# A list scheduler in the kernel's source: weights from traces and eight transfer lanes in place of a table of offsets

## The chip, the cores and the metric

The kernel runs on one core of one Trainium2 chip. The metric is the device time of one execution in microseconds, as the median of several runs. Engines are named as in the profile: PE (TensorE, matmuls), PEld (its weight loads), DVE (VectorE), ACT (ScalarE), POOL (GpSimd) and SP (SyncE, which here issues most transfers). Each engine works off its own instructions in the order in which the program has them.

## What is computed

Two layers on x of shape (4, 256, 64, 64), all in float32. Layer 0 is a Mamba block over 4 x 4096 tokens of 256 channels with an inner width of 512 and 16 states per channel. Layer 1 is a second state-space block, with 8 heads of 64, followed by a mixture of 8 experts in which each token goes to one expert of limited capacity.

```python
# layer 0, per token l (cut)
tokens = x.transpose(0, 2, 3, 1).reshape(B, L, C) @ w_in.T
z = sigmoid(silu(tokens @ w_gate.T + b_gate))
t = layernorm(tokens); xm, zm = split(t @ in_w.T)
xm = silu(causal_conv4(xm)); dt = softplus(...); Bss, Css = ...
h = exp(dt * A) * h + (dt * xm) * Bss          # 512 x 16 states
y = (h * Css).sum(-1) + D * xm
out = tokens + (y * silu(zm) @ out_w.T) * z @ w_out.T + x
# layer 1 (cut)
zxbcdt = rmsnorm(ln(t)) @ W_in.T               # then conv4, silu, softplus
state = state * dA + dt * x B ;  y = state C + D x
t = t + ln(t) + rmsnorm(y * silu(z)) @ W_out.T
# experts (cut)
e = argmax(softmax(ln(t) @ gate_w + gate_b))
t = t + prob * (relu(ln(t) @ w1[e] + b1[e]) @ w2[e] + b2[e])   # up to a capacity per expert
```

## The kernel before

The kernel has three phases. `mixers` does both state-space layers and the routing, `experts` works through blocks of 256 routed tokens, and `turn` transposes the result back into channels-first layout. Only `mixers` is touched here.

`mixers` cuts the 16384 tokens into 64 chunks of 256. A chunk runs through stages, each a Python function: `front0` (input products, first convolution), `mid0` (softplus, and the step sizes, inputs and B and C are written to DRAM in another layout), `scan` (the recurrence of layer 0), `tail0`, `front1` (second layer's products and convolution), `ssd` (its chunked recurrence) and `back1` (output, routing, a scatter of rows to the experts' buffer). Chunk i's layer 0 is recorded together with chunk i-2's `ssd` and `back1`.

A chunk's `scan` has 16 units, four channel groups j by four state groups f. A unit is:

- on ACT, four exponentials into `da` (the decay; three buffers);
- on DVE, the product `ub` = u x B into PSUM (one buffer), a small add into its first column (`ub<-ub,e`, the carry from the chunk before) and the scan itself, `h` (`tensor_tensor_scan`, 1024 columns);
- on ACT, a copy of the last column, `hlast`;
- on POOL, the product `p` = h x C (two buffers), and on PE the sum over states into `py`, which DVE multiplies into `g` once for every two channel groups.

Nothing of this is issued when it is written down. The class `Plan` records every operation as an `Op` with an engine, a weight (its planned duration), the operations that it depends on and a slot (its priority). `Plan.order` then runs a list scheduler: each engine takes, among the operations whose inputs are ready in the plan and whose buffers are free, the one with the lowest slot. `Plan.issue` emits the program in the order of the planned starts. The plan's times decide the order alone; on the chip an instruction starts when its engine gets to it and its semaphores allow.

What the change touches in it:

- The weights, by a formula in each recording method: `mm`, `transpose`, `act`, `copy`, `dve`, `gps`, `scatter`.
- `SIGNAL`, the time from the end of an operation to when another engine can use it; a later operation of the same engine could start at once.
- Two rules for the shared memory port of DVE and POOL: an operation with `port` set does not start while the other engine has one under way, and `p`, recorded with `ride=True`, is placed with the start of a scan (which does not use the port) unless it has waited for `PATIENCE`. `issue` then makes `p` wait for the DVE instruction ahead of that scan.
- `SHIFT`, a table of 140 offsets: `Chunk.at(n)` sets the slot of a chunk's n-th stage step to `n` plus the offset under the step's running number.

Of the kernel before, what the change touches and what calls it, by code (L numbers as in the profile page):

```python
# [20 lines left out]
P = 128  # L21
# [22 lines left out]
TAIL, SSD, BACK = 18, 29, 37  # L44
AHEAD = 4

SHIFT = {
    1: -2.3, 4: 1.4, 5: 0.2, 6: -1.3, 7: -0.3, 8: -0.3, 9: -0.3, 10: -0.3, 11: -0.3, 12: -0.3, 14: -0.3, 15: -0.3,
    16: -0.3, 17: -0.3, 18: -0.3, 19: -0.3, 20: -0.3, 21: -0.3, 22: -0.3, 23: -0.3, 24: -0.3, 25: -0.3, 26: -3.3,
    27: -2.2, 28: 0.2, 29: -0.1, 30: -2.2, 31: -2.2, 32: -2.2, 33: -2.2, 34: -2.2, 35: -2.2, 36: -2.2, 37: 1.2,  # L50
    38: 0.5, 39: -2.2, 40: -2.1, 41: -2.2, 42: -2.7, 43: -2.2, 44: -2.2, 45: -6.0, 46: -2.2, 47: -2.2, 48: -2.2,
    49: -2.2, 50: -2.2, 51: -2.2, 52: -9.4, 53: -2.2, 54: -1.4, 55: -2.2, 56: -2.2, 57: -2.2, 58: -2.2, 59: -2.2,
    60: -4.7, 61: -2.2, 62: -2.2, 63: -2.2, 64: -2.2, 65: -2.2, 66: -2.2, 67: -2.7, 68: -2.2, 69: -2.2, 70: -2.2,
    71: -0.1, 72: -2.2, 73: -2.2, 74: -2.2, 75: -5.9, 76: -4.8, 77: -2.2, 78: -2.2, 79: -2.7, 80: -2.2, 81: -2.2,
    82: -2.2, 83: -2.2, 84: -2.2, 85: -5.2, 86: -2.2, 87: -2.2, 88: -2.2, 89: -2.2, 90: -2.2, 91: -1.4, 92: -2.2,
    93: -2.2, 94: -2.2, 95: -2.7, 96: -2.2, 97: -2.2, 98: -2.2, 99: -2.2, 100: -2.2, 101: -2.2, 102: -2.2,
    103: -2.2, 104: -2.2, 105: -2.2, 106: -2.3, 107: -4.0, 108: -2.0, 109: -2.2, 110: -2.2, 111: -2.2, 112: -2.2,
    113: -1.8, 114: -1.3, 115: 0.9, 116: -0.3, 117: 1.8, 118: -0.3, 119: 0.1, 120: -0.3, 121: -0.3, 123: -0.3,
    124: -0.3, 125: -0.3, 126: 0.6, 127: -1.2, 128: -0.3, 129: -0.3, 130: 0.3, 131: 0.4, 132: -1.4, 133: -0.3,
    134: -0.3, 135: -0.3, 136: 1.6, 137: -0.3, 140: 0.6,  # L60
}
TOK = 4
ROW = TOK + C

# [85 lines left out]
class Plan:  # L150
# [3 lines left out]

    SIGNAL = 0.15
    SPARE = {}
    PATIENCE = 4.0

# [57 lines left out]

    def mm(self, out, left, right, **kw):
        rows, n = out.shape[0], self.width(right)  # L220
        w = max(0.24, n / 550) if rows > 64 else max(0.16, n / 900) if rows > 32 else max(0.15, n / 1500)
        self.note("PE", w, self.nc.tensor.matmul, (out, left, right), kw, (out,), (left, right), join=out.root)

    def transpose(self, out, src, ident):
        w = 0.08 + 0.1 * src.shape[0] / P
        self.note("PE", w, self.nc.tensor.transpose, (out, src, ident), {}, (out,), (src,), join=out.root)

    def act(self, out, src, func, **kw):
        w = 0.2 + self.width(out) / 1200
        self.note("ACT", w, self.nc.scalar.activation, (out, src, func), kw, (out,), (src, *kw.values()))  # L230

    def copy(self, out, src):
        self.note("ACT", 0.2 + self.width(out) / 1200, self.nc.scalar.copy, (out, src), {}, (out,), (src,))

    def acts(self, weight, calls):

# [4 lines left out]
    def dve(self, name, *args, **kw):  # L241
        out, *rest = (*args, *kw.values())
        tensors = [a for a in rest if isinstance(a, Part) or hasattr(a, "ap")]
        n = max(self.width(a) for a in (out, *tensors))
        port = len([a for a in tensors if self.on_sbuf(a) and self.width(a) > 1]) > 1
        if name == "tensor_tensor_scan":
            n, port = 2 * n, False
        op = self.note("DVE", 0.14 + n / 960, getattr(self.nc.vector, name), args, kw, (out,), rest, port=port)
        op.scan = name == "tensor_tensor_scan"
        if op.scan:  # L250
            self.scans.append(op)
# [2 lines left out]
        self.dve("tensor_tensor", out, a, b, op)  # L254

    def gps(self, name, *args, ride=False, **kw):
        w = 0.3 + self.width(args[0]) * 2.02e-3
        f = getattr(self.nc.gpsimd, name)
        self.note("POOL", w, f, args, kw, (args[0],), args[1:], port=True, ride=ride)

# [6 lines left out]
    def scatter(self, out, rows, src, bound):  # L267


        def f(out, rows, src):  # L270
            return self.nc.gpsimd.indirect_dma_start(
                out=out,
                out_offset=bass.IndirectOffsetOnAxis(ap=rows, axis=0),
                in_=src,
                in_offset=None,
                bounds_check=bound,
                oob_is_err=False,
            )

        self.note("POOL", 1.8, f, (out, rows, src), {}, (out,), (rows, src), lag=4.0)  # L280

    def order(self):
# [8 lines left out]
        free = dict.fromkeys(engines, 0.0)  # L293
        port = {"DVE": 0.0, "POOL": 0.0}

        rings, queues, events = {}, {}, [0.0]
# [4 lines left out]
        for op in self.ops:  # L301
            if not op.missing:
                heappush(waiting[op.engine], (0.0, op.seq, op))
        done = 0
        scan = before = last = shared = None

        def room(op, now):
            for root in op.roots:
                if not root.begun:
                    ring, queue = rings.setdefault(root.ring, []), queues[root.ring]  # L310
                    ring[:] = [o for o in ring if o.left or o.until + self.SIGNAL > now]
                    while queue[-1].begun:
                        queue.pop()
                    if len(ring) + (queue[-1] is not root) * self.SPARE.get(root.ring, root.depth) >= root.depth:
                        return False
            return True

        while done < len(self.ops):
# [6 lines left out]
            for e in engines:  # L325
                while waiting[e] and waiting[e][0][0] <= now:
                    _, _, op = heappop(waiting[e])
                    insort(could[e], (op.slot, op.seq, op))
                if free[e] > now:
                    continue  # L330
                for i, (_, _, op) in enumerate(could[e]):

                    if op.ride and not (scan and now - scan.start < 0.2) and now - op.ready < self.PATIENCE:
                        continue
                    if op.port and port["DVE" if e == "POOL" else "POOL"] > now:
                        continue
                    if room(op, now):
                        break
                else:
                    continue  # L340
                del could[e][i]
                for root in op.roots:
                    if not root.begun:
                        root.begun = True
                        rings[root.ring].append(root)
                op.start, op.end = now, now + op.weight + op.lag
                free[e] = now + op.weight
                heappush(events, free[e])
                if op.port:
                    port[e] = free[e]  # L350
                if e == "DVE":
                    scan = op if op.scan else None
                    before, last = last, op
                    if op.port:
                        shared = op
                elif op.ride:
                    op.behind = before if scan and now - scan.start < 0.2 else shared
                for root in op.roots:
                    root.left -= 1
                    root.until = max(root.until, op.end)  # L360
                    if not root.left:
                        heappush(events, root.until + self.SIGNAL)
                for u in op.users:
                    u.missing -= 1
                    late = op.end if u.engine == e and not op.lag else op.end + self.SIGNAL
                    u.ready = max(u.ready, late)
                    if u.ride and not u.missing:
                        heappush(events, u.ready + self.PATIENCE)
                    if not u.missing:
                        heappush(waiting[u.engine], (u.ready, u.seq, u))  # L370
                        heappush(events, u.ready)
                done += 1
# [16 lines left out]
def tile_conv_attn_hybrid(ctx: ExitStack, tc: tile.TileContext, a: dict, out: bass.AP, cap: int, st: int):  # L389
# [41 lines left out]
    def mixers(es):  # L431
# [220 lines left out]
        def silus(*tiles, gates=0):  # L652

            calls = [(nc.scalar.activation, (t, t, AF.Silu), t, t) for t in tiles]

            calls += [(half_tanh, (t[:, :KC],), t[:, :KC], t[:, :KC]) for t in tiles[:gates]]
            calls.append((nc.scalar.preload_act_table_set, (SETS,), None, None))
            r.acts(sum(0.2 + Plan.width(t) / 1200 for t in tiles) / len(calls) + 2.6 / len(calls), calls)

        def inv_sqrt(dst, src, eps, scale=1.0):  # L660

# [871 lines left out]
```

## Time and profile before

| what | us |
|---|---|
| median of 3 runs (lowest, highest) | 6952.74 (6948.43, 6954.37) |
| the profiled execution | 6966.12 |
| its span, first to last instruction | 6964.3 |
| start of the span to the first scan | 109.4 |
| first scan to last scan (64 chunks x 16) | 5615.8 |
| last scan to the last expert's scatter | 1147.8 |
| turning the result | 91.3 |

The page gives each engine's busy time over the whole span; since the phases differ, the stretch of the scans has to be read by itself. A row of waits says how long an engine sat idle ahead of an instruction and what ended the wait. Idle time shorter than 0.15 us is not put into these rows, so a gap that is short but comes thousands of times shows only in the list of instructions in order of time, where each row has its start and its duration. Durations on DVE reach to the end of the write, and the next instruction may start before that.

### The profile page before, as it was taken

To read this page: it belongs to the slowest core of one execution; us is meant where nothing else is said; L and a number is where in the kernel's file an instruction comes from. 1 tells how busy PE (TensorE), PEld (TensorE's weight loads), DVE (VectorE), ACT (ScalarE), POOL (GpSimd) and SP (SyncE) were. 2 spreads that over 40 slices of the span, in tenths; PEclk is the share of its full clock that TensorE was granted. 3 is DMA by queue.
4 is the path that set the end of the run, shared out by engine and by line. 5 is a ranking of instruction groups with operands and counts; after the bars stand their busy time and mean duration, and the time that the engine had idled before them with its cause. 6 is when DMAs were issued, how large, how long until landed. Compare 5 with 4: busy or idle time off the path is not lost. (4 is left out here: it accounts for less than half of the span.)

```text
span 6964.3 us, 114017 instructions
## 1 busy us (share of the span) xinstructions
PE 6084.7 (87%) x37672; PEld 4128.5 (59%) x37672; DVE 5670.3 (81%) x7646; ACT 4892.5 (70%) x12007; POOL 3431.0 (49%) x2632
## 2 busy tenths in 40 slices
PE   5788888888888888888888888888888877999996
PEld 3455555555555555555555555555555546888886
DVE  4899999999999999999999999999999983434443
ACT  4778888888887778788887777878777863333332
POOL 3455555555555555555555555555555552333331
PEclk7899999999888988998898888989888888999998
DMA  6966667666666666666666666666666633555556
GB/s 178 255 172 178 181 178 182 178 178 178 178 177 173 174 172 176 174 176 171 174 178 177 175 178 176 179 177 176 171 175 176 174 106 132 189 194 197 193 191 238
DMA packets 1125137, 1245.56 MB, mean 179 GB/s; under 512 B 111888, under 2 KB 1093652, under 8 KB 1115330
## 3 DMA queue, kind: packets, MB, share of 16 engines
q1 hardware_dynamic: 1083458, 1008.76, 54.9%
q0 software_dynamic: 30000, 210.98, 8.5%
q10 hardware_dynamic: 11088, 18.53, 0.7%
q8 instruction: 299, 4.90, 0.3%
q14 instruction: 292, 2.39, 0.1%
HBM read 919.92 MB, written 311.63 MB: 177 GB/s over the span
## 5 line engine op out<-in xcount | busy, mean ns | idle before, releaser
L378 POOL TENSOR_TENSOR p<-h,bc 128x1024 f32<-128x1024 f32 x1024 | 2420.7, 2364 | 1980.3 <-DVE ub L378 1371.8
L378 DVE TENSOR_TENSOR_SCAN h<-da,ub 128x1024 f32<-128x1024 f32 x1024 | 2341.8, 2287 | 190.5 <-ACT da L378 69.1
L378 ACT ACTIVATE da<-dt,w_m_Alog 128x255 f32<-128x255 f32 x4096 | 1791.1, 500 | 26.1 <-DVE h L378 17.6
L378 DVE TENSOR_TENSOR ub<-u,bc 128x1024 f32<-128x1024 f32 x1024 | 1370.2, 1338 | 23.9 <-DMA dt<-dt_d 11.5
L378 PE MATMUL py<-p,sum 128*32 128x256 f32 x8192 | 719.0, 434 | 255.2 <-POOL p L378 242.9
L378 PE MATMUL b<-t,w_W_in 128*128 128x256 f32 x2304 | 640.2, 424 | 17.6 <-DVE res L378 10.5
L378 ACT COPY hlast<-h 128x4 f32<-128x4 f32 x1024 | 198.7, 194 | 598.7 <-DVE h L378 596.8
L378 PEld LDWEIGHTS py<-p,sum 128*32 128x32 f32 x8192 | 182.0, 114 | 693.9 <-POOL p L378 399.4
L378 PEld LDWEIGHTS b<-t,w_W_in 128*128 128x128 f32 x2304 | 458.7, 208 | 163.8 <-issue 44.2
L378 PE MATMUL a<-t,w_m_in_w 128*128 128x256 f32 x2048 | 549.8, 422 | 3.5 <-DVE t L378 3.5
L1381 PE MATMUL ph<-xt,w 128*128 128x256 f32 x2272 | 517.1, 381 | 11.5 <-DMA w<-in_w_exp_dram,w_at 6.4
L378 PEld LDWEIGHTS a<-t,w_m_in_w 128*128 128x128 f32 x2048 | 415.9, 211 | 149.5 <-issue 61.0
L1392 PE MATMUL po<-w,hid 128*128 128x256 f32 x2272 | 502.0, 379 | 0.0
L1381 PEld LDWEIGHTS ph<-xt,w 128*128 128x128 f32 x2272 | 427.3, 191 | 70.4 <-ACT hid L1383 7.3
L1392 PEld LDWEIGHTS po<-w,hid 128*128 128x128 f32 x2272 | 431.7, 190 | 58.7
L378 PE MATMUL a<-raw,taps_m 128*32 128x256 f32 x2048 | 211.3, 492 | 234.1 <-DMA raw<-raw_d 169.9
L378 PE MATMUL c<-cum,after 128*128 128x512 f32 x512 | 325.7, 724 | 96.8 <-DVE ex L378 89.9
L1358 DVE CAST number<-rows 128x2 uint32<-128x2 f32 x71 | 12.0, 170 | 476.1 <-DMA tok_d<-fixed,number 461.4
L1356 ACT ACTIVATE tn<-rows 128x256 f32<-128x256 f32 x142 | 82.5, 597 | 414.0 <-DMA rows<-buf_d,row_at 413.5
L1404 POOL DMA_INDIRECT tok_d<-fixed,number x142 | 145.9, 1028 | 390.0 <-DVE fixed L1402 307.6
L378 ACT ACTIVATE cum<-upto,da 128x128 f32<-128x128 f32 x1024 | 337.4, 396 | 0.0
L378 ACT ACT_TABLE_LOAD x256 | 328.4, 1283 | 4.5
(237 smaller groups left out, 11087.4 us busy)
## 6 DMA issues: line engine op xcount, KB each, us to landing
raw<-raw_d SPq DMA_DIRECT2D x2048, 128.0 KB
dt<-dt_d SPq DMA_DIRECT2D x1024, 128.0 KB
u<-u_d SPq DMA_DIRECT2D x1024, 128.0 KB
raw_d<-raw SPq DMA_DIRECT2D x128, 518.0 KB
gx_d<-pre SPq DMA_DIRECT2D x64, 1024.0 KB
bc<-bc_d SPq DMA_DIRECT2D x1024, 64.0 KB
gx<-gx_d SPq DMA_DIRECT2D x256, 256.0 KB
dt_d<-mid SPq DMA_DIRECT2D x64, 512.0 KB
```

Source lines behind the costliest of these rows:

```text
L378: op.issued = f(*map(placed, args), **{k: placed(v) for k, v in kw.items()})
L1356: act(tn[:, j], rows[:, j, TOK:], AF.Identity, scale=rows[:, j, 1:2], bias=rows[:, j, 2:3])
L1358: nc.vector.tensor_copy(number, rows[:, :, 3])
L1381: mm(ph, w1[:, k, f * P : (f + 1) * P], xt[:, k], start=k == 0, stop=k == KC - 1)
L1392: mm(po[:, j], hid[:, f, j * P : (j + 1) * P], w2[:, f], start=f == 0, stop=f == KF - 1)
L1404: nc.gpsimd.indirect_dma_start(out=tok_d, out_offset=bass.IndirectOffsetOnAxis(ap=number[:, j : j + 1], axis=0), in_=fixed[:, j], in_offse ...
```

## The change

The table `SHIFT` is emptied, so that a stage's slot is the plain number in the source. The weights are given by other formulas. `SIGNAL` becomes a figure per engine, a second table `BEHIND` says how much later than its source an operation of the same engine may start, and a buffer's free time includes the signal. In the plan SP issues no transfer while eight are under way. No operation is added, removed or changed in its operands.

```diff
-SHIFT = {
-    1: -2.3, 4: 1.4, 5: 0.2, 6: -1.3, 7: -0.3, 8: -0.3, 9: -0.3, 10: -0.3, 11: -0.3, 12: -0.3, 14: -0.3, 15: -0.3,
...
-    134: -0.3, 135: -0.3, 136: 1.6, 137: -0.3, 140: 0.6,
-}
+SHIFT = {}
...
-    SIGNAL = 0.15
+    SIGNAL = {"DVE": 0.13, "ACT": 0.19, "PE": 0.21, "POOL": 0.12}
+    BEHIND = {"DVE": 0.13, "ACT": 0.14, "PE": 0.0, "POOL": 0.13}
+    LANES = 8
...
-        w = max(0.24, n / 550) if rows > 64 else max(0.16, n / 900) if rows > 32 else max(0.15, n / 1500)
+        w = max(0.224, n / 592) if rows > 64 else max(0.12, n / 1100) if rows > 32 else max(0.15, n / 1500)
...
-        w = 0.08 + 0.1 * src.shape[0] / P
+        w = 0.11 if src.shape[0] > 64 else 0.2
...
-        w = 0.2 + self.width(out) / 1200
+        aps = sum(isinstance(v, Part) or hasattr(v, "ap") for v in kw.values())
+        w = 0.06 + self.width(out) / 1130 + 0.09 * aps
...
-        self.note("ACT", 0.2 + self.width(out) / 1200, self.nc.scalar.copy, (out, src), {}, (out,), (src,))
+        self.note("ACT", 0.05 + self.width(out) / 1200, self.nc.scalar.copy, (out, src), {}, (out,), (src,))
...
-        op = self.note("DVE", 0.14 + n / 960, getattr(self.nc.vector, name), args, kw, (out,), rest, port=port)
+        op = self.note("DVE", (0.06 if n > 4 else 0.14) + n / 960, getattr(self.nc.vector, name), args, kw, (out,), rest, port=port)
...
-        w = 0.3 + self.width(args[0]) * 2.02e-3
+        w = 0.15 + self.width(args[0]) * 2.1e-3
...
-        self.note("POOL", 1.8, f, (out, rows, src), {}, (out,), (rows, src), lag=4.0)
+        self.note("POOL", 1.4, f, (out, rows, src), {}, (out,), (rows, src), lag=4.0)
...
-                    ring[:] = [o for o in ring if o.left or o.until + self.SIGNAL > now]
+                    ring[:] = [o for o in ring if o.left or o.until > now]
...
-                if free[e] > now:
+                if free[e] > now or e in lanes and len(landings) >= self.LANES and landings[-self.LANES] > now:
...
+                if e in lanes:
+                    landings.append(op.end)
+                    heappush(events, op.end)
...
-                    root.until = max(root.until, op.end)
+                    root.until = max(root.until, op.end + (0.06 if op.lag else self.SIGNAL[e]))
...
-                    late = op.end if u.engine == e and not op.lag else op.end + self.SIGNAL
+                    late = op.end + (0.06 if op.lag else (self.BEHIND if u.engine == e else self.SIGNAL)[e])
...
-            r.acts(sum(0.2 + Plan.width(t) / 1200 for t in tiles) / len(calls) + 2.6 / len(calls), calls)
+            r.acts(sum(0.06 + Plan.width(t) / 1130 for t in tiles) / len(calls) + 2.6 / len(calls), calls)
```

## The prediction

> **What bounds the kernel now.** I read the page's totals first, then the busy time by stretch, cut where the first and the last scan of VectorE (DVE) stand.
>
> ```profile
> span 6964.3 us, 114017 instructions
> PE 6084.7 (87%) x37672; PEld 4128.5 (59%) x37672; DVE 5670.3 (81%) x7646; ACT 4892.5 (70%) x12007; POOL 3431.0 (49%) x2632
> ```
>
> ```profile
> core 0: us, PE busy (x) PEld busy (x) DVE busy (x) ACT busy (x) POOL busy (x), PEclk, DMA share, GB/s
> 0.00:109.40 109.40, 59.71 (x226) 42.57 (x226) 15.41 (x33) 34.67 (x67) 21.21 (x66) 0.78 0.47 136
> 109.40:5725.20 5615.80, 4886.70 (x31925) 3099.77 (x31925) 5172.81 (x6686) 4481.37 (x11126) 3035.42 (x2197) 0.90 0.67 178
> ```
>
> The change touches only the recorded phase, and 5615.8 us of it lie between the first and the last scan: 64 chunks of 16 scans, 87.75 us a chunk. DVE is busy in 92% of that, PE in 87%, and PE's ends are modelled. What remains, 6966.12 - 5615.8 = 1350.3 us, is start, experts and turning, whose code is the same. The chain of waits that the page prints covers only the end of the run, so for this stretch I go by DVE: its waits first, then its instructions in order of time.
>
> ```profile
> engine line waited for: us in total, times, longest us
> DVE h L378 <- ACT da L378: 69.1, 62, 3.0
> DVE g L378 <- PE py L378: 41.0, 39, 3.1
> DVE xdt L378 <- PE c L378: 35.4, 39, 1.8
> DVE shift L378 <- ACT scale L378: 30.0, 44, 1.0
> DVE stats L378 <- PE b L378: 21.0, 11, 2.9
> ```
>
> ```profile
> 3009.97 1.22 DVE L378 TENSOR_TENSOR ub<-u,bc 128x1024 f32<-128x1024 f32 x1
> 3011.10 0.68 DVE L378 TENSOR_TENSOR xdt<-c,dt 128x512 f32<-128x512 f32 x1
> ...
> 3046.40 0.17 DVE L378 TENSOR_REDUCE red<-ex 128x2 f32<-128x16 f32 x1
> 3046.61 0.17 DVE L378 TENSOR_TENSOR ex<-ex,red 128x16 f32<-128x16 f32 x1
> ...
> 3047.50 1.23 DVE L378 TENSOR_TENSOR ub<-u,bc 128x1024 f32<-128x1024 f32 x1
> 3048.76 0.17 DVE L378 TENSOR_TENSOR ub<-ub,e 128x4 f32<-128x4 f32 x1
> 3049.04 2.29 DVE L378 TENSOR_TENSOR_SCAN h<-da,ub 128x1024 f32<-128x1024 f32 x1
> ```
>
> The listed waits on other engines come to only some 240 us with the smaller rows. The second list shows a loss that no wait row names. When the next instruction does not read the result, it starts before the end of the one in front (3011.10 against 3009.97 + 1.22 = 3011.19; the median is 83 ns early). When it does read it, it starts 34 ns after the end, and a scan 132 ns after. So a pair of neighbours of which one reads the other costs 117 ns, or 215 ns ahead of a scan.
>
> **The change, part by part.** No instruction is added or removed. What changes is the order in which the recorded operations are issued. SHIFT goes, the weights change, and a same-engine reader now counts as ready only 0.13 us after its source. So the cost lies in the two programs' orders, which I laid side by side, engine by engine.
>
> *Gaps on DVE.* Neighbours that read each other, from the first to the last scan: 2819 before, 895 after. By kind: product ub to its first-column add 809 to 303, ub to scan 1003 to 511, small chains (statistics, routing) 1007 to 81. The gross saving is 506 x 0.117 + 492 x 0.215 + 926 x 0.117 = 59 + 106 + 108 = 273 us. Part of it is not had, since a 0.07 us instruction put into a 0.117 or 0.215 us gap leaves the remainder open. Adding the remainders along DVE's own order (its medians, the three distances, no other engine) leaves 458 us of gaps before and 244 after. **Term: -214 us.** Bounds: -273, and 0 if DVE meets waits wherever it comes early.
>
> *Waits for other engines.* I take the DVE work that the order lays between an instruction and the last DVE result that its operand was made from; where it grows, the operand is more likely there. The shift row's grows from 1.13 to 4.70 us (30 us of wait may go), that of the softplus step de from 0.45 to 1.58 (10.5). Finished sets of the decay da ahead of the scan when ACT starts its long silu block: 2.25 to 3.0; two sets ahead at 337 of 1024 scans, then 564. Half of the da row, 35 us, may go. Against that, g falls from 4.1 to 4.7 down to 3.5, and before, py was ready 1.1 us ahead of g at the median but only 0.07 at the lower quarter. Up to 0.95 us for each of 128 g is 122 us. At the median row goes from 10.1 to 7.65 us and state from 3.46 to 1.72, and before, each found its operand only 0.36 us early. Behind a DVE instruction that waits stand the next ub and scan, and behind the scan p and py, so such a wait is paid in full. **Term: 0 us**, freed 75 against some 75 new. Bounds: -75 with nothing new, +200 if g waits in full and state and row take 0.3 us each in 256 places.
>
> *The port that DVE's two-operand products and POOL's product p share.* A ub that runs into p took 1.77 us at the median and 1.23 otherwise, and ub's mean of 1338 ns over the median of 1226 makes 115 us in 1023 of them. p still rides with a scan: it waits for something no more than two instructions ahead of one in 1020 of 1024 cases before and in 1016 after. But 59 scans now carry two p and 59 none, and a second p, starting 2.4 us late, lies on the next ub: 59 x 2.3 = 136 us if no other instruction fills it. **Term: 0 us**, bounds -115 and +136; I take the middle since both orders place p at the scan.
>
> *SP's queue.* All 6241 recorded transfers stay, in a new order; eight in flight is now part of the plan. DVE work from issue to first reader: dt 7.8 to 11.2 us, bc 10.4 to 11.9, u 17.8 to 17.0, the tap loads raw 6.6 to 4.9 (first convolution) and 9.4 to 7.7 (second). A raw that lands late holds PE's queue and with it py and g. This is the third rival; in the sum it is 0, with PE's idle time of 5615.8 - 4886.7 = 729 us as its cover.
>
> *More waits as instructions of their own.* On DVE 2583 before, 2797 after; at the 34 ns by which a reader lags its source, +7 us.
>
> Do the new weights fit? A scan is planned at 2.193 us and its successor starts 2.204 after it; ub 1.127 and 1.13; a 256-column matmul 0.432 and two passes of 216 ns. Too short are da (0.376 against 0.399) and the silu block, which leaves out a 0.65 us tanh in both kernels. So most waits that the plan avoids should also be absent on the chip.
>
> **Sum:** -214 + 0 + 0 + 0 + 7 = -207 us on the profiled execution's 6966.12: 6759. The median of the timed runs is 6952.74, 13.4 lower, so 6746; I say 6745.
>
> One rule speaks against the change. The Trainium skill, in "VectorE: DVE Perf Modes", sections "The DRAIN you can't avoid" and "Rules for kernel authors", says that each DVE operation is followed by a flush of the pipeline whatever it is chained to, and advises fewer operations rather than another order. By that the first term would be 0 and the kernel would stay near 6953. This trace disagrees as far as it goes, with 83 ns early against 34 ns late depending on who reads; the same page concedes that an operation that is not held starts earlier.
>
> **The rivals.** (1) *The waits and collisions shrink too.* The exact weights may free the 75 us and two thirds of the 115: 6746 - 150 = 6596. For it are the da lead and shift; against it the tighter g, row and state. (2) *The gaps are filled and DVE then waits instead.* Per chunk the gain is 3.3 us, and DVE's waits are 240/64 = 3.8; if they nearly double, nothing is left: 6953. For it: most distances to PE's results are shorter. Against: list order puts something else in front where an operand isn't ready. (3) *Slower: raw comes late and PE's queue becomes the bound.* Place: the 512 groups of four tap matmuls, 8 a chunk. Their loads lose 1.7 us of lead. If all of it turns into PE idle time, PE needs 4886.7 + 512 x 1.7 = 5757 us, longer than the stretch now: 5757 + 1350 - 13 = 7094. It decides from 1.42 us a group (729/512) upward. For it is the row below, with loads already late; against it are dt and bc, which gain lead, and the shortest raw lead, which fits a plan of eight transfers in flight.
>
> ```profile
> PE a L378 <- DMA raw<-raw_d: 160.7, 84, 4.7
> ```
>
> (4) *The order is neutral*, because each DVE instruction pays its gap whoever reads it: 6953.
>
> **How the numbers follow.** Chances: forecast 0.54, (1) 0.18, (2) 0.10, (3) 0.13, (4) 0.05. What can be told from no change is 0.2%, 14 us. Faster: 0.54 + 0.18 + half of (2) = 0.77; same: 0.03 of (2) and 0.03 of (4) = 0.06; slower: 0.17. The forecast's own range is 6640 to 6850. Low end: the sum with the freed waits and most of the collisions gone, 6746 - 75 - 95 = 6576, say 6580. High end: the sum with +200 of waits and a third of the second-p cost, 6746 + 200 + 45 = 6991, say 6990; that holds (2) and (4) and leaves out most of (3).
>
> **What would show it.** In the new profile: ub's first-column add and the scan with small instructions between them, the first-to-last-scan stretch near 5410 us (84.5 a chunk), DVE above 93% busy there, the shift row gone, da's smaller, g's about as now. Wrong if the stretch shrinks with the pairs still neighbours, or if the pairs are parted and the wait rows of g, row or raw have grown by 200 us.

## The result, and the profile after

The changed kernel takes 6787.23 us (median of 4 runs, 6774.94 to 6789.17) against 6953.25 us for the kernel before (4 runs, 6948.43 to 6954.37): a ratio of 0.9759, with a 95% interval of 0.9742 to 0.9776. Forecast were 6745 us. The profiled execution took 6786.87 us.

The page's totals of the kernel after:

```profile
span 6785.2 us, 114276 instructions
PE 5984.4 (88%) x37672; PEld 4045.8 (60%) x37672; DVE 5545.7 (82%) x7646; ACT 4859.2 (72%) x12007; POOL 3494.2 (51%) x2632
```

Its busy time by stretch, the second row from the first to the last scan:

```profile
core 0: us, PE busy (x) PEld busy (x) DVE busy (x) ACT busy (x) POOL busy (x), PEclk, DMA share, GB/s
0.00:111.90 111.90, 60.70 (x226) 44.12 (x226) 15.49 (x34) 34.49 (x67) 21.38 (x67) 0.85 0.44 127
111.90:5546.20 5434.30, 4781.51 (x31933) 3015.68 (x31933) 5052.55 (x6689) 4449.84 (x11128) 3098.71 (x2197) 0.93 0.73 184
```

All of the gain lies in that row: 5434.3 us for what took 5615.8, so 84.9 us a chunk instead of 87.75. What lies outside it came to 1350.3 us before and is 6786.87 - 5434.3 = 1352.6 now. DVE is busy in 93.0% of the row (5052.55 / 5434.30), before in 92.1%. The busy share hides the gaps. Rows of independent neighbours overlap by some 83 ns, so parting the pairs took time out of the busy total as well (5172.81 to 5052.55), although the instructions stayed the same.

DVE's instructions in order of time, kernel after (start, duration, then what it is):

```profile
1002.46 1.22 DVE L371 TENSOR_TENSOR ub<-u,bc 128x1024 f32<-128x1024 f32 x1
1003.60 0.48 DVE L371 SCALAR_TENSOR_TENSOR row<-c,rr,res 128x264 f32<-128x264 f32 x1
1004.00 0.15 DVE L371 TENSOR_TENSOR ub<-ub,e 128x4 f32<-128x4 f32 x1
1004.07 0.41 DVE L371 BATCH_NORM_STATS2 stats<-row 128x6 f32<-128x256 f32 x1
1004.40 2.26 DVE L371 TENSOR_TENSOR_SCAN h<-da,ub 128x1024 f32<-128x1024 f32 x1
```

A `row` now lies between `ub` and the add into its first column, and a `stats` between the add and the scan, where before each followed directly. From `ub` to the scan it is 1.94 us. Not every place is parted like this: 303 adds and 511 scans still follow directly.

DVE's waits in the stretch, kernel after:

```profile
engine line waited for: us in total, times, longest us
DVE xdt L371 <- PE c L371: 80.2, 137, 2.6
DVE state L371 <- PE c L371: 58.1, 50, 1.2
DVE gm L371 <- PE c L371: 40.0, 48, 2.6
DVE pre L371 <- PE c L371: 20.7, 48, 1.9
DVE mid L371 <- ACT mid L371: 20.0, 51, 3.0
...
DVE h L371 <- ACT da L371: 4.8, 4, 3.6
```

The rows that led before are nearly gone: the decay `da` 69.1 to 4.8, `shift` 30.0 to none, and `g` on `py` 41.0 to 2.5. In their place stand results of PE's group `c` (the second layer's products), and most come once a chunk: 50 waits of `state`, 48 of `gm`, 51 of `mid`. All rows of the list add up to 255 us before (the forecast reckoned with some 240) and 273 after.

PE's own waits in the stretch, kernel after, the two rows that bear on the third rival:

```profile
engine line waited for: us in total, times, longest us
PE py L371 <- POOL p L371: 326.3, 241, 6.1
...
PE a L371 <- DMA raw<-raw_d: 14.3, 5, 8.5
```

The tap loads that PE waited 160.7 us for are down to 14.3.

For the comparisons below I kept one account for every kernel. Each time from a DVE start to the next DVE start, from the first to the last scan, is split into four: the instruction's own work (its median duration in the kernel before, less the 83 ns by which an independent successor comes early); waits, where DVE sat idle 0.15 us or more ahead of the next one (with the 83 ns of lead lost there, so the lists' 255 and 273 us are 278 and 305 here); gaps, what is lost by shorter distances; and stretching, what an instruction took above its median. It is worked out from the traces, in us:

```
                          total   own work  waits   gaps  stretching
before                   5615.7       4761    278    444         133
after                    5434.3       4764    305    255         111
after minus before       -181.4         +3    +27   -189         -22
```

### The profile page after: what moved, and what is told of

Read it like the earlier page. It is cut to its first block, busy times and chain, and to the rows that moved or that the text cites. A ratio compares the mean times of both kernels' runs of the same rounds, so it can differ in the third digit from the quotient of the medians.

```text
span 6785.2 us, 114276 instructions
## 1 busy us (share of the span) xinstructions
PE 5984.4 (88%) x37672; PEld 4045.8 (60%) x37672; DVE 5545.7 (82%) x7646; ACT 4859.2 (72%) x12007; POOL 3494.2 (51%) x2632
## 5 line engine op out<-in xcount | busy, mean ns | idle before, releaser
L371 ACT ACTIVATE da<-dt,w_m_Alog 128x255 f32<-128x255 f32 x4096 | 1830.7, 502 | 0.5 <-issue 0.5
L371 DVE TENSOR_TENSOR ub<-u,bc 128x1024 f32<-128x1024 f32 x1024 | 1269.1, 1239 | 20.2 <-DMA u<-u_d 11.3
L371 PE MATMUL py<-p,sum 128*32 128x256 f32 x8192 | 689.6, 411 | 334.1 <-POOL p L371 326.3
L371 PE MATMUL b<-t,w_W_in 128*128 128x256 f32 x2304 | 581.5, 393 | 65.1 <-ACT raw L371 26.1
L371 PEld LDWEIGHTS b<-t,w_W_in 128*128 128x128 f32 x2304 | 420.8, 191 | 230.6 <-ACT raw L371 90.3
L371 PE MATMUL a<-t,w_m_in_w 128*128 128x256 f32 x2048 | 496.6, 391 | 4.5 <-DVE t L371 4.5
L371 PEld LDWEIGHTS a<-t,w_m_in_w 128*128 128x128 f32 x2048 | 377.0, 191 | 125.8 <-issue 50.6
L1376 ACT ACTIVATE hid<-ph,w 128x256 f32<-128x256 f32 x426 | 187.4, 468 | 143.7 <-PE ph L1374 143.1
```

The lines of the kernel that those rows point to most:

```text
L371: op.issued = f(*map(placed, args), **{k: placed(v) for k, v in kw.items()})
L1376: act(hid[:, f], ph, AF.Relu, bias=b1[:, f : f + 1])
```

## The experiments

The kernel before was run beside every experiment on the same chip (medians 6944.76 to 6951.82 us), and each ratio stands against those runs.

### Which part of the change carries the gain

**e1: the changed kernel without the 0.13 us.** All weights, signals and lanes of the change stay; only a reader on DVE counts as ready again at the end of its source.

```diff
-    BEHIND = {"DVE": 0.13, "ACT": 0.14, "PE": 0.0, "POOL": 0.13}
+    BEHIND = {"DVE": 0.0, "ACT": 0.14, "PE": 0.0, "POOL": 0.13}
```

> The changed kernel, but in the plan a DVE operation may again follow its DVE source at once; all else of the change stays. Its order has 2799 neighbouring pairs on DVE that read each other (before 2819, changed kernel 895). Theory (the gain is the gaps between such neighbours): the short gaps on DVE go from 255 us back to some 450 and the time from 6787 to 6950-6990 us. Rival (the exact weights, the signal times or the missing table brought the gain, the gaps cost nothing on the path): it stays within 30 us of 6787.

Measured: 6943.28 us (10 runs), ratio 0.9995 [0.9985, 1.0005], 7 us below the expected range. One figure takes back the whole gain. Neighbours of which one reads the other are 2799 again, and the gaps 464 us. DVE in order of time, kernel e1:

```profile
3012.08 1.22 DVE L371 TENSOR_TENSOR ub<-u,bc 128x1024 f32<-128x1024 f32 x1
3013.34 0.17 DVE L371 TENSOR_TENSOR ub<-ub,e 128x4 f32<-128x4 f32 x1
3013.61 2.29 DVE L371 TENSOR_TENSOR_SCAN h<-da,ub 128x1024 f32<-128x1024 f32 x1
```

The add starts 0.04 us after the end of `ub`, the scan 0.10 us after that of the add; from `ub` to the scan it is 1.53 us. Had `row` (0.48 us) and `stats` (0.41 us) been put elsewhere among instructions that don't read each other, each would take its duration less the 83 ns, 0.40 and 0.33 us. With the 1.53 us that makes 2.26, and the kernel after does the five in 1.94: 0.32 us less, where the two distances of the forecast, 0.117 and 0.215 us, make 0.33.

It also settles two side questions. PE's wait for `raw` is 13.0 us in e1 (window from 112 to 5400 us), as short as after, and the time is that of before: the `raw` row was covered. And e1's waits of DVE, 235 us, are 43 below those of before without a faster kernel: its gaps take back 20 us of that, and most of the rest is no gain of the order, since the profiled execution of before lay 13 us above its median, and before itself took 8 us less on e1's chip.

**e2: the kernel before with the 0.13 us on DVE alone.** The old weights and the table of offsets stay.

```diff
-                    late = op.end if u.engine == e and not op.lag else op.end + self.SIGNAL
+                    late = op.end + (0.13 if e == "DVE" else 0.0) if u.engine == e and not op.lag else op.end + self.SIGNAL
```

> The kernel before with its old weights and its table of offsets, and one thing more: in the plan a DVE operation may follow its DVE source only 0.13 us later. Its order has 1004 neighbouring pairs that read each other. Theory: the gaps fall by some 190 us as in the changed kernel, waits may grow since the table was made for another order: 6750-6870 us. Rival: within 30 us of 6953.

Measured: 6849.57 us, ratio 0.9856 [0.984, 0.9873]. The gaps fall by 231 us, 42 more than in the change, but the waits rise by 110. DVE's waits, kernel e2, from 112 to 5400 us:

```profile
engine line waited for: us in total, times, longest us
DVE gm L378 <- PE c L378: 98.9, 61, 3.6
DVE shift L378 <- ACT scale L378: 78.6, 53, 1.5
DVE h L378 <- ACT da L378: 51.3, 59, 4.3
DVE state L378 <- ACT dend L378: 37.1, 32, 4.9
```

`gm` stood at 12.0 before. So the 0.13 us makes the gain in either kernel. How much comes back as waits differs with the rest of the plan; which part of it decides that, e2 doesn't tell, since weights, table and lanes differ together.

**e3: the changed kernel without the eight lanes.**

```diff
-    LANES = 8
+    LANES = 10**6
```

> The changed kernel with no limit to transfers under way in the plan. Gaps as in the changed kernel (901 pairs). Theory: the eight lanes order SP's queue and give dt and bc their lead, but are not where the gain is: 6770-6830 us. Rival (loads in the wrong order hold PE and DVE): above 6870, with rows of waits for DMA on DVE or PE grown by 80 us or more.

Measured: 6805.96 us, 0.9799 [0.9783, 0.9815]. The lanes are worth some 19 us by the times, 28 by the ratios. PE's wait for `raw` goes to 43.2 us (14.3 with lanes), but the time is lost on DVE, where the waits grow from 305 to 374 us, `gm` to 118.3.

**e4: the changed kernel with the old table of offsets, and e5: the kernel before without it.**

```diff
-SHIFT = {}
+SHIFT = {
+    1: -2.3, 4: 1.4, 5: 0.2, 6: -1.3, 7: -0.3, 8: -0.3, 9: -0.3, 10: -0.3, 11: -0.3, 12: -0.3, 14: -0.3, 15: -0.3,
...
+}
```

e5 is the same edit the other way round, in the kernel before.

> The changed kernel with the old table of offsets put back; 872 pairs, gaps as in the changed kernel or 20 us less. Theory: the offsets suit the old weights alone, so they bring nothing here: 6770-6860 us, any difference to be found in the rows of waits. Rival (the table carried a gain of its own that the change gave up): below 6750.

> The kernel before with the table of offsets emptied and nothing else changed; 2857 neighbouring pairs on DVE that read each other, gaps as before. Tells what the table was worth. Theory (gaps, not offsets): the table moved waits alone and was worth less than 60 us: 6940-7010 us, gaps 445-460 us, the rest in the rows of waits. Rival (the table hid much, and the change had to win it back): above 7020.

Measured: e4 6796.08 us, 0.9782 [0.9766, 0.9798], an interval that overlaps the change's own; e5 6949.49 us, 1.0007 [0.9997, 1.0018]. The 140 offsets were worth nothing that shows, in either kernel. They do move work: in e4 the gaps fall to 199 us and the waits rise to 417.

### Is filling the gaps enough?

**e6: the order of before, then filled by hand.** After the list scheduler, the program looks at each pair of DVE neighbours of which one reads the other, and moves in front of the reader the first of the next 15 DVE operations that is no scan, does not use the shared port and has its inputs issued already.

```diff
+    def filled(self):
...
+            if a in b.deps:
+                for n in range(k + 1, min(k + 16, len(line))):
+                    x = line[n]
+                    if x.scan or x.port or a in x.deps:
+                        continue
+                    if any(at[d] >= at[b] for d in x.deps) or any(born[r] >= at[b] for r in x.roots):
+                        continue
+                    del line[n]
+                    line.insert(k, x)
...
-        for op in self.order():
+        for op in self.filled():
```

> The kernel before, its own order with its table and weights, and afterwards small DVE operations that do not use the shared port moved forward into gaps, where all their sources are already issued: 2102 neighbouring pairs instead of 2819, summed gaps about 70 us less. No plan is made anew. Theory: the time falls by the gaps alone, 45-75 us, to 6870-6910 us. Rival (a gap is worth nothing, the new plan as a whole is what helps): within 20 us of 6945.

Measured: 7258.58 us, 1.0447 [1.0426, 1.0469]. It is a miss, and a useful one: the gaps do fall, by 79 us, and the waits rise by 363. DVE's waits, kernel e6, from 112 to 5400 us:

```profile
engine line waited for: us in total, times, longest us
DVE pre L403 <- PE c L403: 263.8, 105, 4.9
DVE stats L403 <- PE b L403: 89.5, 46, 3.7
```

An input that has been issued is not an input that is there. `pre` was pulled ahead of its matmul's end, 105 times at 2.5 us, and everything behind it on DVE waited along. Parting a pair pays only if the plan knows when the filler's own input comes.

### How far can the plan's figures be pushed?

The traces show figures that the change still has wrong. A scan needs some 0.1 us more behind its source than another reader; a 0.07 us operation cannot fill that; the 64-row matmuls, transposes and the silu block take longer than planned. Six variants of the changed kernel take these up. None of them came out in the range expected of it: e7, e8 and e10 were 34, 36 and 50 us below it, e9 was 5 above, e11 and e12 186 and 231 above.

**e7: a scan's reader distance, and tiny operations at their true width.**

```diff
-        op = self.note("DVE", (0.06 if n > 4 else 0.14) + n / 960, getattr(self.nc.vector, name), args, kw, (out,), rest, port=port)
+        op = self.note("DVE", 0.06 + n / 960, getattr(self.nc.vector, name), args, kw, (out,), rest, port=port)
...
+                    if u.scan and e == "DVE":
+                        late += 0.1
```

> The changed kernel with DVE's own times nearer to the trace: a small operation is planned at 0.06 us and not 0.14, and a scan may follow its source only 0.23 us later and not 0.13. Summed gaps 27 us less than the changed kernel's. Theory: 6745-6790 us, short gaps near 225 us; what goes against it are new waits. Rival (the plan's finer times no longer matter): within 10 us of 6787 or above.

Measured: 6711.07 us, 0.9662 [0.9645, 0.9678]. The gaps fall by 28 us and the waits by 40; `ub` runs into `p` again (87 us of stretching, 14 after).

**e8: weights of PE and ACT nearer to the trace.**

```diff
-        w = max(0.224, n / 592) if rows > 64 else max(0.12, n / 1100) if rows > 32 else max(0.15, n / 1500)
+        w = max(0.224, n / 592) if rows > 64 else max(0.14, n / 1000) if rows > 32 else max(0.15, n / 1500)
...
-        w = 0.11 if src.shape[0] > 64 else 0.2
+        w = 0.15 if src.shape[0] > 64 else 0.3
...
-        w = 0.06 + self.width(out) / 1130 + 0.09 * aps
+        w = 0.06 + self.width(out) / 1130 + 0.07 * aps + 0.045 * hasattr(kw.get("scale"), "shape")
...
-            r.acts(sum(0.06 + Plan.width(t) / 1130 for t in tiles) / len(calls) + 2.6 / len(calls), calls)
+            r.acts(sum(0.06 + Plan.width(t) / 1130 for t in tiles) / len(calls) + (2.6 + 0.65 * gates) / len(calls), calls)
```

> The changed kernel with weights of other engines nearer to the trace: 64-row matmuls 0.14 us and not 0.12, transposes 0.15 and not 0.11, a scale operand on ACT 0.115 and not 0.09, the tanh counted in the silu block. Tests where the new waits on PE (xdt, state, gm, pre: 199 us) come from. Theory (they come from weights that are too short): these rows fall by half and the time to 6700-6770 us. Rival (they come from PE passes that run at half rate at some places, which no fixed weight foresees, or from the order that happened to come out): the rows move among themselves, 6770-6830 us.

Measured: 6663.51 us, 0.9583 [0.9561, 0.9605]. The gaps are much as after (244 us), the waits 103 us fewer.

**e9: e7 and e8 together.**

> The nearer weights of PE and ACT and the nearer gap times of DVE together. Gaps as in the changed kernel (236 us on the added-up order, the changed kernel 236, e8 249, e7 209). Theory (each correction takes away its own loss, but list order does not add them): 6630-6690 us. Rival (the two gains add, 76 and 124): below 6610.

Measured: 6695.17 us, 0.9636 [0.9611, 0.966]. The two gains do not add up; it is slower than e8 alone. Gaps and waits are each some 14 us below e8's, and 46 us more of stretching (`ub` 75, `state` 31) outweigh that.

**e10: only PE's two weights of e8** (its first two pairs of lines).

> The changed kernel with PE's weights alone nearer to the trace (64-row matmuls and transposes), ACT's left. Theory (the new waits were DVE on PE, so PE's weights carry most of e8's 124 us): 6670-6720 us, the rows xdt, state and pre halved. Rival (ACT's silu block and scale operands carry it): 6750-6800 us.

Measured: 6620.2 us (6615.57 to 6625.42), 0.9528 [0.9504, 0.9551]: the fastest here, below both kernels. DVE's waits, kernel e10, from 112 to 5400 us:

```profile
engine line waited for: us in total, times, longest us
DVE gm L371 <- PE c L371: 42.0, 54, 3.1
DVE pre L371 <- PE c L371: 18.7, 14, 5.5
DVE xdt L371 <- PE c L371: 14.6, 51, 0.3
```

The gaps, 248 us, are those of the kernel after. The gain over it is in the waits, 141 us in all against 305: `xdt` from 80 to 15 and `state` gone from the top.

**e11: e8 with POOL's weight nearer to the trace as well, and e12: e11 with e7.**

```diff
-        w = 0.15 + self.width(args[0]) * 2.1e-3
+        w = 0.2 + self.width(args[0]) * 2.11e-3
```

> e8_weights with POOL's product planned at 2.36 us and not 2.30, as the trace has it. Its summed gaps come out 37 us below e8's (212 against 249 on the added-up order). Theory: decay's and ub's stretch by p (78 us in e8) falls by a third, gaps by 35: 6590-6650 us. Rival (60 ns in 2.3 us change nothing but the draw of the order): 6640-6690 us.

> e11_pool and the nearer gap times of DVE together, all corrections at once; 218 us of gaps on the added-up order. Theory: among the best, 6580-6650 us. Rival (the plan is at its limit, further corrections only move the waits): 6650-6700 us.

Measured: e11 6836.06 us, 0.9846 [0.9818, 0.9874]; e12 6880.6 us, 0.9898 [0.987, 0.9925]. Both are misses: 0.06 us more in POOL's product cost 173 us against e8. DVE's waits, kernel e11, from 112 to 5400 us:

```profile
engine line waited for: us in total, times, longest us
DVE gm L371 <- PE c L371: 204.5, 104, 4.1
DVE pre L371 <- PE c L371: 75.7, 58, 3.5
```

and PE's, in the same kernel and window:

```profile
engine line waited for: us in total, times, longest us
PE py L371 <- POOL p L371: 247.7, 90, 3.9
PE c L371 <- ACT dend L371: 196.0, 54, 3.8
```

DVE's `gm` waits for PE's `c`, and PE's `c` waits, 54 times for some 3.6 us, for ACT's `dend`. In e8 that row of PE is 37.2 us. So the order of e11 seems to have put one ACT step of the second layer late in most of the 64 chunks, and the three engines to pass that on; this is read from the rows, and no run takes it away. e12 has the same two rows on DVE (`gm` 186.7, `pre` 108.9), but there PE waits for `dend` only 10.7 us in all: the cause seems to be another, and was not found.

The account of all of them, in us; "pairs" are DVE neighbours that read each other:

```
                      time   pairs   waits  gaps  stretching
before              6953.25   2819     278   444         133
e5 no offsets       6949.49   2857     234   464         149
e1 no 0.13          6943.28   2799     235   464         136
e6 filled           7258.58   2102     641   365         138
e2 before + 0.13    6849.57   1004     388   213         139
after               6787.23    895     305   255         111
e3 no lanes         6805.96    901     374   230          90
e4 offsets back     6796.08    872     417   199          80
e7 scan distance    6711.07    916     265   227         111
e8 weights          6663.51   1040     202   244         116
e9 e7 + e8          6695.17   1164     188   230         162
e10 PE weights      6620.20    935     141   248         123
e11 e8 + POOL       6836.06    787     361   232         122
e12 e11 + e7        6880.60   1016     483   208          77
```

Two things are to be seen. With the 0.13 us in the plan the gaps are 199 to 255 us, in all ten kernels; without it 444 to 464, and 365 in e6, whose pairs were parted afterwards. And the waits among those ten reach from 141 to 483 us, which accounts for most of their differences in time. No figure that was edited explains that spread by its size.

## Why the prediction was right, and where it was off

The forecast stood on its main step, and that step held: the gain comes from parted neighbours on DVE. Its 6759 us for the profiled execution were 28 below the 6786.87 measured, and 6787.23 lies within the forecast's own 6640 to 6850. That the sum came so near is in part luck: the steps missed by +25, +27, -22 and -7 us, which partly cancel. By steps:

- **Gaps on DVE, -214: the mechanism was right, the size 25 too large.** The account gives -189. The remainders had been added up to 458 us before and 244 after, without other engines; on the chip they were 444 and 255. e1 shows the cause by removing it alone, e2 by adding it alone.
- **Waits for other engines, 0: nearly right as a sum (+27), but by other rows than named, so the sum was luck.** The freed ones came as reasoned, and more fully: `da` 64 us rather than half of 69, `shift` 30. Of the new ones, `state` came (58 us), but `row` is not among the larger rows, and `g` went the other way, from 41.0 to 2.5, though less DVE work lies ahead of it. `xdt`, `gm`, `pre` and `mid`, for which no distance was worked out, made the rest. The method, DVE work between an instruction and the DVE result behind its operand, fails for them: their operands depend on how far PE and ACT have come in the second layer's chain. The statement that `g` would stay about as now is wrong.
- **The shared port, 0: -22.** `ub`'s mean fell from 1338 to 1239 ns, so the lower bound of -115 was nearly reached for it (stretching 115 to 14), and the cost moved to others: `decay` 48 us, `mid` 17. The kernel after shows it at POOL and DVE, here POOL in order of time,

```profile
1043.63 2.37 POOL L371 TENSOR_TENSOR p<-h,bc 128x1024 f32<-128x1024 f32 x1 [1.26 <-DVE ub L371]
...
1046.38 2.36 POOL L371 TENSOR_TENSOR p<-h,bc 128x1024 f32<-128x1024 f32 x1
```

  and DVE at the same time:

```profile
1047.73 2.09 DVE L371 TENSOR_TENSOR decay<-decay,gm 128x1024 f32<-128x1024 f32 x1
...
1050.35 1.22 DVE L371 TENSOR_TENSOR ub<-u,bc 128x1024 f32<-128x1024 f32 x1
```

  `decay` starts inside the second `p`, which ends at 1048.74, and takes 2.09 us instead of 1.22; the `ub` behind it is free. The second `p` does fall on what follows, as reckoned, but that is often `decay`, not `ub`, and it costs less than the upper bound had it: 53 slowed `decay` lost some 0.9 us each, where the forecast put 2.3 us on each of 59, though its own row for `ub` (1.77 against 1.23) showed 0.54.
- **SP's queue, 0: right.** The cover named, PE's idle time, was not needed: the `raw` row shrank. Lead by DVE work had spoken for later loads, and was no guide. From 112 to 5400 us the row is 154.3 us before and 49.6 with the table emptied alone (e5); in the changed kernel it is 14.3, 43.2 without the lanes (e3) and 66.0 with the table put back (e4).
- **More wait instructions, +7: nothing of that size can be told apart.** With the own work at +3 and the rest of the kernel at +2 the account closes: 25 + 27 - 22 - 7 + 3 + 2 = 28.
- **The step from the profiled execution to the median, -13.4,** did not recur. The profiled execution of before lay 13 us above its median, that of after at its median (6786.87 against 6787.23). This is a further 14 of the 42 us by which 6745 fell short.

The signs: first to last scan 5434.3 us for "near 5410", DVE busy 93.0% for "above 93%", `shift` gone, `da` smaller, and `row` and `stats` around the add, as said; only `g` was not. None of the signs of being wrong came.

The rivals: (1), 6596, did not come with this change, but e10 with 6620 shows that the waits can go that far, though it was not through the collisions (123 us of stretching). (2) is what happened in e6 and, for half of the gain, in e2; in the change itself the waits rose by 27 only. (3) fell with the `raw` rows. (4) fell with e1: the same instructions in another order, 156 us apart (6943.28 against 6787.23). The Trainium skill, "VectorE: DVE Perf Modes", section "The DRAIN you can't avoid", has the next operation wait for the emptied pipeline after every one, and adds that one that is not held starts earlier. The first sentence alone would make the order neutral, and these runs disagree with that; of the order of operations the page gives no rule.

What stays open is why the waits come out as they do. They follow the whole order, and a list scheduler's order shifts throughout when one weight moves by 0.06 us (e8 to e11). e8, e9 and e10 with PE's nearer weights have the fewest waits, but e11 and e12 have those weights too and have many. So it is not shown that a nearer weight is a better one, and e10 is a good order that was found, not one that was derived. For the two largest rows of the kernel after, `xdt` and `state`, the trace gives a lead, the halved clock of PE, which the last section shows.

## What to carry to other kernels

Put the distance between an instruction and its reader on the same engine into the scheduler's model: 0.13 us for some 2800 pairs was worth 1.4% with the old weights and table (e2) and the whole 2.4% of the change with the new ones (e1), and 140 hand-set offsets nothing that shows. Don't fill such gaps without the arrival times of the fillers' inputs, since one early instruction on an in-order engine costs more than many gaps. Treat the rest of a list schedule as a draw: build several plans with slightly different weights, measure them, and keep the fastest, here 6620.2 us.

## What the hardware showed beyond that

- **The granted clock of PE changes with the order, and the time does not simply follow it.** The mean over the span is 0.906 before and 0.908 in e1, 0.934 after, and 0.941 in e8 and e10. The mean 256-column matmul `b<-t,w_W_in` went from 424 to 393 ns. But e11 has 0.935 at 6836 us, and e5, the kernel before with its table emptied, has 0.924 and 389 ns without any gain in time (6949.49 us), so the higher clock brought nothing there. What in the order sets the clock wasn't tried.
- **Matmul groups at half pace are stretches of halved clock, and the order moves them.** The traces have the clock at 1.0 or 0.5 and nothing between; at 0.5 it is for 1312 us before, 895 after and 780 in e10. All of the 290 `b<-t,w_W_in` over 600 ns before fall into such stretches, and 257 of the 260 `a<-xin,w_cen` after. So the mean of `a<-xin,w_cen` is 402 ns before, 404 in e1 and 405 in e10, but 533 after. PE and then DVE, kernel after, around such a group:

```profile
2009.16 2.97 PE L371 MATMUL a<-xin,w_cen 128*128 128x256 f32 x8
```

```profile
2014.09 0.69 DVE L371 TENSOR_TENSOR xdt<-xdt,dend 128x512 f32<-128x512 f32 x1 [1.05 <-PE c L371]
...
2018.19 0.42 DVE L371 TENSOR_TENSOR state<-state,c 128x256 f32<-128x256 f32 x1 [1.18 <-PE c L371]
```

  Eight matmuls take 2.97 us instead of 1.99, the clock is 0.50 from 2007.8 to 2011.1 us, and some microseconds later DVE waits twice for a `c` of PE. In 47 of the 64 chunks this group has matmuls over 600 ns, and in 40 of these both waits follow within 14 us; in none of the 17 others do both. On the mean these waits are 2.2 us in each of the 47 chunks and 0.6 in each of the 17. By that some 75 us of the kernel's waits go with the halved clock (47 x 1.6, an estimate). That the one causes the other is an argument from the order in time; no run tried it.
- **A collision at the shared port costs half to most of a microsecond:** `decay` 2.09 against 1.22 us over `p`, `ub` 1.77 against 1.23 in the kernel before. A `p` that started first still takes 2.36 us. The Trainium skill, "SBUF — State Buffer", section "Who interferes with whom", calls the pair of ports that the two engines share an exclusive lock; the rows fit that.
